# Seven small products for two large ones in an experts' first layer, other dispatch steps, and another filler

## The chip, the cores and the metric

The kernel runs on one core of one Trainium2 chip. The metric is the device time of one execution in microseconds (us), as the median of several runs. The engines are named as the profile names them: PE (TensorE, matrix products; PEld are its weight loads), DVE (VectorE), ACT (ScalarE), POOL (GpSimd) and SP (SyncE, which issues most transfers). PSUM is the memory that products are written to, in eight banks.

## The reference, cut to what matters

4096 tokens of width 512 pass through an attention over 3202 context rows and then through a mixture of eight experts, two for each token. Only the second half is touched by the change:

```python
def _L0_ffn_ref(x, w_router, b_router, w1, b1, w2, b2):
    ...
    cap = max(1, int(CAP_FACTOR * n / e))
    ...
    buf = jnp.zeros((e, cap, d), x.dtype).at[e_flat, posc].add(jnp.where(keep[:, None], xf[tok], 0.0))
    h = jax.nn.gelu(jnp.einsum('ecd,edf->ecf', buf, w1) + b1[:, None, :], approximate=False)
    out = jnp.einsum('ecf,efd->ecd', h, w2) + b2[:, None, :]
    og = out[e_flat, posc]
    w = jnp.where(keep, g_flat, 0.0).astype(x.dtype)
    y = jnp.zeros((n, d), x.dtype).at[tok].add(w[:, None] * og)
```

A token has a slot at each of its experts, `cap` is 640 slots, and the hidden width is 2048. All of it is computed in 32-bit floats.

## The kernel before, in words

There are three stages. The first is the attention, 1438 us, and the change doesn't touch it. The second ("routing") makes the attention's output for 32 tiles of 128 tokens, chooses experts and slots and writes the rows to the experts' slots in memory. The third runs the eight experts one after the other.

**Routing.** The tiles are taken in steps, `STEPS`, of 4, 4, 4, 4, 4, 3, 3, 2, 2, 2 tiles. A tile is 16 matmuls on PE (`tile_mm`, L1757), an add on DVE (`x1`) and a square sum on ACT. `scale` makes the step's `rstd` on POOL, `choose` picks the two experts on DVE and ACT and yields a mask, `place` counts with two matmuls (`pos`, L1872 and L1873) and gives each row its slot, and `dispatch` (POOL, an indirect transfer for each tile and choice, 64 in all) writes the rows. The order of these is written out by hand with `tc.issue_after`: a step is chosen while the next step's tiles are computed. `send(n)` issues n of the waiting dispatches. After the last tile, PE has no tiles left. There `idle_work` (L94) issues products of constants, 7 before the last `pos` and 1 behind it, and `first_expert_in` issues four products with a tile of zeros (L2152), the transposes of the first expert's five row tiles (`bps`, L85), more idle products, and the first expert's early products (`early_product`, L2118).

**An expert.** Its first layer is W1 (512 by 2048) times the 640 rows' transpose. It is done by the Strassen-Winograd scheme on blocks: `w1_forms` gives A11, A12, A22, S1, S2, A21 (in place S3), S4, and `XS` gives B11, B21, B22, T1, T2, T3, T4. With `HC` = 320 columns, `hidden(e, idx)` for idx 0 to 7 (`h`, `f` = half and quarter of the hidden width) makes seven products of two matmuls each, 128x128 by 128x320, on banks X, Q, Y, Z, W = 0, 1, 2 or 3, 4, 5. PE's order in an idx is X (0), Q (3), Y (4), X (1), Z (5), Y (6), W (2). The scheme's running sums are made by ACT, which copies a finished bank to the next one (Y<-X, L2210; p5<-Q, L2213; Z<-Y, L2216; W<-Z, L2223), where the next product is accumulated. DVE adds p5 to the two blocks that need it (L2224, L2226), and ACT applies the gelu, some of it in the next idx (`owed`). In expert 0, idx 0 to 3, the products X are done early, in the filler's time, and `early` holds them.

In between, DVE makes forms that are needed later: `w1_sums` (S1, S2, S3, S4 of the next idx's weights), and `left` and `right` (forms of the second layer). `dv`, `ac`, `ld` and `mm` each chain their instructions, so that every engine's order is that of the program. An in-order engine that waits for one instruction holds all behind it.

**The second layer** (`output`, `inner`, `deep`, `plain`, `rest`) uses two levels of the same scheme, with 128-column matmuls at its deeper level, whose forms DVE makes in 128x512 pieces. The next expert's rows are transposed inside it.

SP's queue loads the weights: `load_w1(e, h)` halves into two buffers in turn, `load_w2`, and `rows_in` for the next expert's rows.

Of the kernel before, what the change touches and what calls it, by code (L numbers as in the profile page):

```python
# [6 lines left out]
F32 = mybir.dt.float32  # L7
# [7 lines left out]
P = 128  # L15
# [5 lines left out]
def gated_layer(ctx, tc, x, x_t, ctxt, ctxt_t, ctxt_c, ctxt_r, g_xattn, g_ffn, w_sim, w_sim_r, b_sim, W_qv, W_qv_t, b_qv, b_qv_c, w_router, b_router, w1, b1, w2, b2, out):  # L21
# [37 lines left out]
    bsim = const.tile([P, 1], F32, name="bsim")  # L59
    gx = const.tile([P, 1], F32, name="gx")  # L60
    gf = const.tile([P, 1], F32, name="gf")
    zeros = const.tile([P, P], F32, name="zeros")
    nc.gpsimd.memset(zeros, 0.0)
    tgx, tgf = gx, gf

    qT_d = [dram.tile([P, DC, TG], F32, name=f"qT_d{g}", tag=f"qT_d{g}") for g in range(NG)]
# [1595 lines left out]
    with ExitStack() as s2:  # L1662
# [54 lines left out]
        scatters, middle, late = [], [], []  # L1717


        STEPS, sizes = [], [G] * (NT // G - 3) + [3, 3, 2, 2, 2]  # L1720
        for n in sizes:
            t = STEPS[-1][-1] + 1 if STEPS else 0
            STEPS.append(list(range(t, t + n)))
# [19 lines left out]
        def tile_mm(s, i):  # L1743
            t = s.tiles[i]
            g, q = divmod(t, 4)
            if g not in qTs:
                qTs[g] = sb.tile([P, DC, TG], F32, name=f"q2T{g}", tag="q2T")
                ld = nc.sync.dma_start(qTs[g], qT_d[g])
            r = sb.tile([P, 2, BW], F32, name=f"r2_{t}", tag="r2", bufs=6)
            ld = nc.sync.dma_start(r, r_d[t])  # L1750
            if t in (NT - 3 * G, NT - 1):
                with tc.issue_after(ld.ins):
                    load_w1(0, 0) if t < NT - 1 else load_w2(0, 0)
            ps = ps_mm.tile([P, 2, 512], F32, name=f"x1p{t}", tag="mm")
            for j in range(2):
                for c in range(DC):
                    mm = nc.tensor.matmul(  # L1757
                        ps[:, j, :B1], qTs[g][:, c, q * P : (q + 1) * P], W1[:, c, j, :], start=(c == 0), stop=(c == DC - 1)
                    )
            x1 = sb.tile([P, D], F32, name=f"x1_{t}", tag="x1", bufs=G + 2)  # L1760
            with tc.issue_after(chosen[-1]) if s.n == 2 and i else ExitStack():
                stt(
                    x1.rearrange("p (j d) -> p j d", j=2), ps[:, :, :256], tgx, r[:, :, :256], ALU.mult, ALU.add,
                    accum_out=s.sum[:, i : i + 1],
                )

            junk = sb.tile([P, D], F32, name=f"jx{t}", tag="jx", bufs=2)
            sq = nc.scalar.activation(
                junk, x1, AF.Square, scale=-float(D), bias=s.sum[:, i : i + 1], accum_out=s.ssd[:, i : i + 1]
            )  # L1770
            with tc.issue_after(sq.ins):
                nc.scalar.dma_start(out[t * P : (t + 1) * P, :], x1)

            l_ = s.lg[:, i, :]
            stt(
                l_.rearrange("p (j e) -> p j e", j=2), ps[:, 0, 256:B1].rearrange("p (j e) -> p j e", j=2), tgx,
                r[:, :, 256:], ALU.mult, ALU.add,
            )
            s.ldone = stt(l_, ps[:, 1, 256:B1], sd[:, t : t + 1], l_, ALU.mult, ALU.add)
            s.x1.append(x1)  # L1780
            return mm
# [7 lines left out]
        def choose(s):  # L1789
# [42 lines left out]


            s.g2 = T("gtwo", [P, n])
            nc.scalar.activation(s.g2, mx[:, 1, :], AF.Exp)
            s.gs = T("gs", [P, n])
            red(s.gs, gate, AX.X, ALU.add)
            for i, x1 in enumerate(s.x1):
# [83 lines left out]

        placed, chosen, w_ops = [], [], []

        idle = ps_id.tile([P, D], F32, name="idle", tag="idle")
        prev, s, scaled = None, begin(0), []
# [13 lines left out]
        for g in range(len(STEPS)):  # L1942
# [6 lines left out]
            if s.n > 2:  # L1949
                with tc.issue_after(mm.ins):  # L1950
                    place_prev()
                if s.n < G:
                    with tc.issue_after(scaled[-1].ins):
                        send(1)
                if s.n < G:

                    if not w_ops:
                        w_ops = w1_sums(0, 0)
                    with tc.issue_after(prev.placed.ins):
                        w_ops.pop(0)()  # L1960
                for i in range(ahead, s.n):
                    tile_mm(s, i)
            sc = scale(s)
            scaled.append(sc)
            if s.n == 2:
                with tc.issue_after(mm.ins):
# [12 lines left out]
                s.lift = small("lift", [P, s.n, E])  # L1979
                stt(s.lift[:, 0, :], cnt, 1.0 / P, second, ALU.mult, ALU.max)  # L1980
            with tc.issue_after(sc.ins):
                send(5 if s.next is None or s.next.n == 2 else 7 if s.n < G else 8)
            prev, s = s, s.next
        choose(prev)
        with tc.issue_after(idle_work(mm, 7).ins):
            place_prev()
        idle_work(prev.counted, 1)
        with tc.issue_after(prev.placed.ins):
            w_sum = w_ops.pop(0)()
        send(len(routed))  # L1990


# [5 lines left out]
    with ExitStack() as s3:  # L1998
# [112 lines left out]
        def early_product(second, f, B, cols, after, last=True):  # L2111

            A = [w1_forms(0, 0)[second][:, k, f * P : (f + 1) * P] for k in range(2)]
            pa = banks[2 + f][:, :HC]
            early[f] = sets[0][f].rearrange("p a b -> p (a b)")[:, :HC]
            for k in range(2):
                with tc.issue_after(after.ins):
                    after = nc.tensor.matmul(  # L2118
                        pa[:, cols], A[k], B[k][:, cols], start=False, stop=bool(second) and k == 1, skip_group_check=True
                    )  # L2120
            if not second:
                nc.scalar.copy(early[f][:, cols], pa[:, cols])
            elif last:
                tail["ac"] = nc.scalar.activation(hT[:, 0, f, :HC], pa, AF.Gelu, bias=b1_t[:, f : f + 1])
            return after
# [4 lines left out]
        def first_expert_in():  # L2130

            behind = None
            for s in range(NST):
# [13 lines left out]
                if behind is None:  # L2147

                    behind = prev.counted
                    for i in range(2, 6):  # L2150
                        with tc.issue_after(behind.ins):
                            behind = nc.tensor.matmul(  # L2152
                                banks[i], zeros, ident.unsqueeze(1).to_broadcast([P, 4, P]), start=True, stop=True
                            )
                        if i == 2:
                            with tc.issue_after(behind.ins):
                                ps = transposed(ps_tr, xb_of[0, s], f"bps0_{s}")
                            behind = moved[-1]
                else:
                    with tc.issue_after(behind.ins):  # L2160
                        ps = transposed(ps_tr, xb_of[0, s], f"bps0_{s}")
                dst = bT[:, :, s * P : (s + 1) * P]
                if s == NST // 2:
                    nc.scalar.copy(dst[:, :2, :], ps[:, :2, :])
# [1 line left out]
                        w_ops.pop(0)()  # L2166
                else:
                    (nc.vector.tensor_copy if s % 2 else nc.scalar.copy)(dst, ps)
                if s:
                    behind = idle_work(moved[-1], s, 2) if s <= NST // 2 else moved[-1]  # L2170
                cols = slice(0, P) if s == 0 else slice(P, HC)
                for q, f in {0: ORDER, NST // 2: ORDER[:5], NST - 1: ORDER[5:]}.get(s, ()):
                    B = [bT[:, k, :HC] for k in ((2, 3) if q else (0, 1))]
# [14 lines left out]

        stored, owed = [], []

        def hidden(e, idx):

            h, f = divmod(idx, KQ)
            col = e * NF + h * KH + f
            lo, hi = hT[:, 0, idx, :], hT[:, 1, idx, :]
            b_lo, b_hi = b1_t[:, col : col + 1], b1_t[:, col + KQ : col + KQ + 1]
            A = [[a[:, k, f * P : (f + 1) * P] for k in range(2)] for a in w1_forms(e, h)]
            X, Q, Y, Z, W = (banks[i][:, :HC] for i in (0, 1, 2 + idx % 2, 4, 5))
            p5 = p5s[idx % 2]
            there = e == 0 and f in early and h == 0  # L2200

            def product(ps, k, start=False):
                for i in range(2):
                    mm(ps, A[k][i], XS[{2: 6, 6: 2}.get(k, k)][i], start and i == 0, i == 1)

            if there:
                ac(lambda: nc.scalar.copy(Y, early.pop(f)))  # L2207
            else:
                product(X, 0, True)
                ac(lambda: nc.scalar.copy(Y, X))  # L2210
            product(Q, 3, True)
            ac(*owed[:1])
            ac(lambda: nc.scalar.copy(p5, Q))  # L2213
            ac(*owed[1:2])
            product(Y, 4)
            ac(lambda: nc.scalar.copy(Z, Y))  # L2216
            ac(*owed[2:])
            owed.clear()
            if not there:
                product(X, 1)  # L2220
                ac(lambda: nc.scalar.activation(lo[:, :HC], X, AF.Gelu, bias=b_lo))
            product(Z, 5)
            ac(lambda: nc.scalar.copy(W, Z))  # L2223
            dv(lambda: tt(hi[:, HC:], Z, p5, ALU.add))  # L2224
            product(Y, 6)
            dv(lambda: tt(lo[:, HC:], Y, p5, ALU.add))  # L2226
            product(W, 2)
            owed.extend([
                lambda: nc.scalar.activation(hi[:, HC:], hi[:, HC:], AF.Gelu, bias=b_hi),
                lambda: nc.scalar.activation(lo[:, HC:], lo[:, HC:], AF.Gelu, bias=b_lo),  # L2230
                lambda: nc.scalar.activation(hi[:, :HC], W, AF.Gelu, bias=b_hi),
            ])


        lo, hi = hT[:, 0], hT[:, 1]
# [86 lines left out]
        for e in range(E):  # L2322
# [23 lines left out]
            for idx in range(2 * KQ):  # L2346
                if more and idx == 2:
                    ld(*[lambda s=s: rows_in(e + 1, s) for s in range(NST - 1)])
                hidden(e, idx)
                if more and idx == KQ - 1:  # L2350
                    ld(lambda: load_w1(e + 1, 0))
                if 1 <= idx <= 4:
                    dv(*w1_sums(e, 1, idx - 1))
                if idx in (2, 4, 6):
                    dv(left(1, idx - 2, idx), left(3, idx - 2, idx))
                if idx == 3:
                    dv(right(1, 0, 4))
                if idx == 5:
# [172 lines left out]
```

## Time and profile before

| what | us | from |
|---|---|---|
| median of 3 runs (2563.48 to 2563.97) | 2563.72 | times |
| profiled execution, its own time | 2565.51 | times |
| profiled execution, span | 2563.7 | page |
| attention, to 1438.20 | 1438.2 | stretches |
| routing, 1438.20 to 1574.00; PE busy 129.62 | 135.8 | stretches |
| last `pos` to the first product of L2029, 1574.00 to 1591.45; PE busy 17.45 | 17.45 | stretches |
| experts, 1591.45 to 2558.00; PE busy 962.95 | 966.55 | stretches |
| one expert, 1707.61 to 1829.13 | 121.5 | timeline |

The granted clock of PE was 0.998 of full speed over the span. The page counts records: a matmul on 32-bit floats leaves two of them. A matmul's record lasts longer than the distance to the next one, since matmuls are pipelined; what a matmul costs in a stream is the distance from one start to the next. "x8" is a group of eight records; a bracket names the idle time before the group and what ended it.

### The profile page before, as it was taken

How to read it: one execution, taken by the hardware profiler on the slowest of the kernel's cores; microseconds unless marked ns; L12 is line 12 of the kernel's file. 1: busy time of each engine (PE TensorE's matmuls, PEld its weight loads, DVE VectorE, ACT ScalarE, POOL GpSimd, SP SyncE). 2: the span in 40 equal slices, each digit the busy share in tenths (PEclk: the TensorE clock that was granted, in tenths of full speed). 3: DMA queues.
4: the chain of work that ended last, by engine and by line, in shares of the span. 5: the costliest groups of instructions: out<-in, count | busy, mean ns of one | idle time of the engine just before them, and what ended most of it. 6: DMA issues, size and time to landing. Idle time of an engine off the chain costs nothing.

```text
span 2563.7 us, 36624 instructions
## 1 busy us (share of the span) xinstructions
PE 2543.1 (99%) x13964; PEld 2196.9 (86%) x13964; DVE 1844.5 (72%) x3670; ACT 693.2 (27%) x1459; POOL 275.9 (11%) x400
## 2 busy tenths in 40 slices
PE   9999999999999999999999999999999999999999
PEld 7788888998988989989989886787888878787978
DVE  8887965977877868759668666767675858484937
ACT  1112302223123123132230244323233232313140
POOL 0101220001001001000000066010101010101010
PEclk9999999999999999999999999999999999999999
DMA  7568795875976857759758795231314141414120
GB/s 260 197 214 299 270 346 168 288 255 177 315 232 207 284 192 263 258 180 304 244 166 281 274 350 202 83 128 66 132 67 156 46 160 38 161 42 156 50 99 21
DMA packets 198399, 488.99 MB, mean 191 GB/s; under 512 B 22462, under 2 KB 79102, under 8 KB 196176
## 3 DMA queue, kind: packets, MB, share of 16 engines
q1 hardware_dynamic: 151984, 386.37, 44.7%
q0 software_dynamic: 21696, 59.07, 6.4%
q10 hardware_dynamic: 24544, 41.21, 4.4%
q8 instruction: 110, 1.80, 0.3%
q14 instruction: 65, 0.53, 0.1%
HBM read 397.40 MB, written 97.52 MB: 193 GB/s over the span
## 4 chain that ended last, share of the span: by engine, by line
PE 88%; issue 5%; DVE 5%; POOL 1%; DMA 1%; ACT 0%; POOLq 0%; SPq 0%; another core or an unknown queue 0%; DVEq 0%; ACTq 0%
PE bank L2029 31%; PE bank L763 21%; PE bank L986 13%; PE bank L1155 6%; PE bank L1512 5%; PE x1p L1757 3%; PE bank L1256 2%; PE p7d L1512 1%; PE p4d L1512 1%; PE bank L815 1%; PE v L1256 1%; DVE SM L1025 1%; PE bank L992 1%; DVE hqT L1192 1%; PE bps L2105 1%
## 5 line engine op out<-in xcount | busy, mean ns | idle before, releaser
L763 PE MATMUL bank<-Qp,kt 128*128 128x256 f32 x1344 | 305.2, 379 | 0.0
L763 PEld LDWEIGHTS bank<-Qp,kt 128*128 128x128 f32 x1344 | 254.4, 190 | 34.1
L2029 PE MATMUL bank<-w,hT 128*128 128x256 f32 (+1 forms) x1280 | 260.7, 359 | 0.7 <-ACT u L2408 0.7
L2029 PEld LDWEIGHTS bank<-w,hT 128*128 128x128 f32 x1280 | 223.8, 190 | 27.4 <-ACT u L2408 1.1
L763 PE MATMUL bank<-q,kt 128*128 128x256 f32 x1008 | 231.3, 379 | 0.0
L2029 PE MATMUL bank<-bT,w 128*128 128x320 f32 x736 | 218.8, 433 | 2.0 <-ACT bank L2216 1.6
L763 PEld LDWEIGHTS bank<-q,kt 128*128 128x128 f32 x1008 | 191.5, 190 | 26.0
L2224 DVE TENSOR_TENSOR hT<-bank,l 128x320 f32<-128x320 f32 x64 | 31.5, 492 | 253.4 <-ACT bank L2223 253.4
L986 PE MATMUL bank<-dt,vf 128*128 128x128 f32 x1680 | 204.8, 275 | 0.0
L986 PEld LDWEIGHTS bank<-dt,vf 128*128 128x128 f32 x1680 | 196.0, 192 | 0.0
L2029 PEld LDWEIGHTS bank<-bT,w 128*128 128x128 f32 x736 | 139.0, 190 | 60.6 <-ACT bank L2216 3.1
L2029 PE MATMUL bank<-XT,w1s 128*128 128x320 f32 x512 | 148.4, 433 | 0.0
L806 DVE TENSOR_TENSOR M<-M,E_all 128x1024 f32<-128x1024 f32 x80 | 97.8, 1223 | 47.8 <-ACT E_all L723 46.4
L2029 PEld LDWEIGHTS bank<-XT,w1s 128*128 128x128 f32 x512 | 97.2, 190 | 40.6 <-ACT bank L2207 0.4
L2397 POOL DMA_INDIRECT out<-acc,ti x40 | 39.6, 990 | 819.2 <-DVE acc L2342 812.5
L1757 PE MATMUL x1p<-W,q2T 128*128 128x264 f32 x512 | 119.8, 396 | 0.5 <-DVE p1d L1527 0.5
L1757 PEld LDWEIGHTS x1p<-W,q2T 128*128 128x128 f32 x512 | 98.8, 195 | 18.0 <-DVE p1d L1527 0.9
L719 DVE TENSOR_TENSOR E_all<-bank,p5s 128x512 f32<-128x512 f32 x42 | 28.9, 689 | 114.5 <-ACT bank L718 114.5
L893 DVE TENSOR_TENSOR E_all<-E_all,mb 128x1024 f32<-128x1024 f32 x84 | 101.2, 1211 | 10.3 <-ACT mb L868 10.3
L986 PE MATMUL bank<-E_all,vf 128*128 128x128 f32 x828 | 106.5, 275 | 0.0
L894 ACT ACTIVATE E_all<-E_all 128x1024 f32<-128x1024 f32 x84 | 88.8, 1057 | 49.8 <-DVE E_all L893 49.3
L986 PEld LDWEIGHTS bank<-E_all,vf 128*128 128x128 f32 x828 | 99.8, 192 | 0.3
(602 smaller groups left out, 4755.9 us busy)
## 6 DMA issues: line engine op xcount, KB each, us to landing
vf<-vf_d SPq DMA_DIRECT2D x122, 768.0 KB
kt<-kt_d SPq DMA_DIRECT2D x84, 512.0 KB
w<-in_w SPq DMA_DIRECT2D x16, 2048.0 KB
w<-in_w SPq DMA_DIRECT2D x32, 1024.0 KB
kt<-in_ctxt_t SPq DMA_DIRECT2D x84, 384.0 KB
wp<-wt_d SPq DMA_DIRECT2D x56, 520.0 KB
buf_d<-zero SPq DMA_DIRECT2D x80, 129.0 KB
xb<-buf_d SPq DMA_DIRECT2D x39, 258.0 KB
```

The lines of the kernel that those rows point to most:

```text
L763: nc.tensor.matmul(ps[:, jl, :], kts[j][:, KSLOT[p], k, :], B[p][:, k, :], start=start and jl == 0 and k == 0, stop=stop and k == 1, skip_ ...
L806: tt(M, M, e[:, :, h], ALU.max)
L893: live[g]["last"] = tt(e, e, m, ALU.subtract)
L894: live[g]["exp"] = nc.scalar.activation(e, e, AF.Exp)
L986: nc.tensor.matmul(ps, a[:, j, :], rhs[r][:, j, :], start=start and j == 0, stop=j == NP - 1 and (rest is None or add is None), skip_group ...
L1155: nc.tensor.matmul(ps[b], vt[:, j - i * JH, b * P : (b + 1) * P], right(j) if j < NJ else right_c, start=start and j == 0 and b == 0, stop ...
L1256: mm = nc.tensor.matmul(acc[k][:, b, :], a[:, b * P : (b + 1) * P], r, start=start and b == 0, stop=stop, skip_group_check=True,)
L1512: nc.tensor.matmul(ps[m], A[p][:, k, m * P : (m + 1) * P], wt[:, k, :], start=start and k == 0, stop=stop and k == DC - 1, skip_group_chec ...
L1757: mm = nc.tensor.matmul(ps[:, j, :B1], qTs[g][:, c, q * P : (q + 1) * P], W1[:, c, j, :], start=(c == 0), stop=(c == DC - 1))
L2029: return chained("pe", lambda: nc.tensor.matmul(ps, a, b, start=start, stop=stop, skip_group_check=True))
L2224: dv(lambda: tt(hi[:, HC:], Z, p5, ALU.add))
L2397: sc = nc.gpsimd.indirect_dma_start(out=out[:, :], out_offset=rows_of(ti, s), in_=accs[s][:, :], in_offset=None, bounds_check=N - 1, oob_i ...
```

## The change

It has three parts.

1. *Split.* In the first layer, idx 0 to 5, products 6 (S4 by B22) and 2 (A22 by T4) are no longer made by two matmuls of 320 columns each. For every two neighbouring idx (a pair, 0 to 2), each of these two products is one block product of 256 rows (of the hidden width), 256 (of the model width) and 320 columns, and is computed by seven products of 128x128 by 128x160 with the scheme once more (`parts`). `deep_w` and `deep_x` make its forms on DVE, four adds each, in buffers of the second layer's sets. A part runs in idx 1 (product 6 of pair 0), 2 (product 2 of pair 0), 3, 4, 5, 6; in each, its pieces `first`, `second`, `third` stand between the idx's other products. The three regions X', W', Q' of a part share one bank of the transposes' pool, and Y', Z' share bank 5 (bank 3 at idx 6). Two copies on ACT carry the running sums (Y'<-X', Z'<-Y'), and four adds on DVE put the part onto the rows of hT; its gelus come an idx later. In expert 0's idx 1 to 3, PE's order becomes X', Q', W', Y (4), Y', X', Q (3), Z', Y', Z (5).
2. *Steps.* 4, 4, 4, 4, 3, 3, 3, 3, 2, 2 instead of 4, 4, 4, 4, 4, 3, 3, 2, 2, 2, with other numbers of dispatches sent at each step; the first two tiles' `x1` of every step of fewer than four wait for the choice of the step before. The sums of the first expert's weights move from the steps to the tail.
3. *Filler.* `idle_work` issues 11 instead of 7 products of constants, then 4 instead of 1; the four products with zeros, and the tile `zeros`, go; two more follow the first transposes. A gelu on one column is put behind the last choice's exponential.

Beside these, `load_w1(e + 1, 0)` moves from idx 3 to idx 4, and the `left` forms from idx 2, 4, 6 to idx 4, 6, 7.

```diff
-        STEPS, sizes = [], [G] * (NT // G - 3) + [3, 3, 2, 2, 2]
+        STEPS, sizes = [], [G] * (NT // G - 4) + [3, 3, 3, 3, 2, 2]
...
-            with tc.issue_after(chosen[-1]) if s.n == 2 and i else ExitStack():
+            with tc.issue_after(chosen[-1]) if s.n < G and i < 2 else ExitStack():
...
-                send(5 if s.next is None or s.next.n == 2 else 7 if s.n < G else 8)
+                send(len(routed) if s.next is None else 4 if s.n == 2 else 7)
             prev, s = s, s.next
         choose(prev)
-        with tc.issue_after(idle_work(mm, 7).ins):
+        with tc.issue_after(prev.last_exp.ins):
+            nc.scalar.activation(small("gelu", [P, 1]), ones[:, 0:1], AF.Gelu)
+        with tc.issue_after(idle_work(mm, 11).ins):
             place_prev()
-        idle_work(prev.counted, 1)
-        with tc.issue_after(prev.placed.ins):
-            w_sum = w_ops.pop(0)()
+        idle_work(prev.counted, 4)
+        w_ops = w1_sums(0, 0)
...
-                    for i in range(2, 6):
-                        with tc.issue_after(behind.ins):
-                            behind = nc.tensor.matmul(
-                                banks[i], zeros, ident.unsqueeze(1).to_broadcast([P, 4, P]), start=True, stop=True
-                            )
...
-                if s:
-                    behind = idle_work(moved[-1], s, 2) if s <= NST // 2 else moved[-1]
+                behind = idle_work(moved[-1], s or 2, 2 if s else 4) if s <= NST // 2 else moved[-1]
...
+        DEEP_IDX = 6
+        HH = HC // 2
...
+        def deep_x(k):
+            b, (t1, t2, t4, t3) = x_of[k]
+            b11, b12, b21, b22 = (b[:, c, d : d + HH] for c in range(2) for d in (0, HH))
+            return [
+                lambda: tt(t1, b12, b11, ALU.subtract),
+                lambda: tt(t2, b22, t1, ALU.subtract),
+                lambda: tt(t3, b22, b12, ALU.subtract),
+                lambda: tt(t4, b21, t2, ALU.subtract),
+            ]
+        def deep_w(e, k, pair):
...
+            return [
+                lambda: tt(s1, a21, a22, ALU.add),
+                lambda: tt(s2, s1, a11, ALU.subtract),
+                lambda: tt(a21, a11, a21, ALU.subtract),
+                lambda: tt(s4, a12, s2, ALU.subtract),
+            ]
+        def parts(e, k, pair, c_bank):
+            XWQ = ps_tr.tile([P, DC, P], F32, name=f"d{e}_{k}{pair}", tag="tr").rearrange("p c t -> p (c t)")
+            X, W, Q = (XWQ[:, i * HH : (i + 1) * HH] for i in range(3))
+            YZ = banks[c_bank][:, : 2 * HH]
+            Y, Z = YZ[:, :HH], YZ[:, HH:]
...
+            def first():
+                mm(X, a11, b11, True, True)
+                ac(lambda: nc.scalar.copy(Y, X))
+                mm(Q, s1, t1, False, True)
+                mm(W, a22, t4, False, True)
+            def second():
+                mm(Y, s2, t2, False, True)
+                ac(lambda: nc.scalar.copy(Z, Y))
+                mm(X, a12, b21, False, True)
+            def third():
+                mm(Z, s3, t3, False, True)
+                mm(Y, s4, b22, False, True)
...
+            split = idx < DEEP_IDX
+            if 1 <= idx <= DEEP_IDX:
+                k, pair = ("6", idx // 2) if idx % 2 else ("2", idx // 2 - 1)
+                part = parts(e, k, pair, 5 if split else 2 + (idx + 1) % 2)
...
+            if not split:
+                product(Y, 6)
+                dv(lambda: tt(lo[:, HC:], Y, p5, ALU.add))
+                product(W, 2)
...
-                if more and idx == KQ - 1:
+                if more and idx == KQ:
                     ld(lambda: load_w1(e + 1, 0))
                 if 1 <= idx <= 4:
                     dv(*w1_sums(e, 1, idx - 1))
-                if idx in (2, 4, 6):
-                    dv(left(1, idx - 2, idx), left(3, idx - 2, idx))
+                if idx == 0:
+                    dv(*deep_w(e, "6", 0), *deep_x("6"), *deep_w(e, "2", 0), *deep_x("2"))
+                if idx == 1:
+                    dv(*deep_w(e, "6", 1), *deep_w(e, "2", 1))
+                if idx == 4:
+                    dv(*deep_w(e, "6", 2), *deep_w(e, "2", 2))
+                if idx in (4, 6, 7):
+                    k = (0, 2, 4)[(4, 6, 7).index(idx)]
+                    dv(left(1, k, k + 2), left(3, k, k + 2))
```

## The prediction

> **What bounds the kernel now.** I read the busy totals, then the chain of waits, then the groups that belong to the diff.
>
> ```profile
> PE 2543.1 (99%) x13964; PEld 2196.9 (86%) x13964; DVE 1844.5 (72%) x3670; ACT 693.2 (27%) x1459; POOL 275.9 (11%) x400
> ...
> PE 88%; issue 5%; DVE 5%; POOL 1%; DMA 1%; ACT 0%; POOLq 0%; SPq 0%; another core or an unknown queue 0%; DVEq 0%; ACTq 0%
> ...
> L2029 PE MATMUL bank<-bT,w 128*128 128x320 f32 x736 | 218.8, 433 | 2.0 <-ACT bank L2216 1.6
> L2224 DVE TENSOR_TENSOR hT<-bank,l 128x320 f32<-128x320 f32 x64 | 31.5, 492 | 253.4 <-ACT bank L2223 253.4
> ```
>
> TensorE sets the time: a matmul removed is worth its own issue time, and a wait put in front of a matmul costs its full length. The two halves of one expert differ on VectorE (columns: stretch, length, then busy time of PE, PEld, DVE, ACT, POOL):
>
> ```profile
> 1707.61:1768.00 60.39, 60.39 (x227) 42.66 (x226) 26.68 (x56) 28.16 (x63) 6.95 (x7) 1.00 0.43 157
> 1768.00:1829.13 61.13, 61.13 (x430) 57.68 (x428) 56.34 (x112) 8.23 (x26) 3.06 (x4) 1.00 0.15 53
> ```
>
> The first layer (`hidden`, first row) leaves VectorE idle for 33.7 us, the second layer almost nothing. So extra VectorE work in `hidden` is affordable as a sum, and only its order can hurt. The timeline of one block gives the durations (columns: start, duration):
>
> ```profile
> 1716.23 2.32 PE L2029 MATMUL bank<-XT,w1s 128*128 128x320 f32 x8
> 1716.43 0.41 ACT L2210 COPY bank<-bank 128x320 f32<-128x320 f32 x1 [2.82 <-PE bank L2029]
> ...
> 1718.38 2.32 PE L2029 MATMUL bank<-bT,w 128*128 128x320 f32 x8
> ...
> 1720.54 1.24 PE L2029 MATMUL bank<-bT,w1s 128*128 128x320 f32 x4
> 1720.79 0.41 ACT L2223 COPY bank<-bank 128x320 f32<-128x320 f32 x1 [0.60 <-PE bank L2029]
> 1721.23 0.49 DVE L2224 TENSOR_TENSOR hT<-bank,l 128x320 f32<-128x320 f32 x1 [6.47 <-ACT bank L2223]
> ```
>
> Eight records take 1718.38 - 1716.23 = 2.15 us, 269 ns each; a program matmul is two. ScalarE's copy begins 0.25 us after the product has ended (1720.79 against 1720.54). VectorE's add on the same bank begins 0.03 us after that copy's end: accesses to one bank are put in a row. And at one place ScalarE's copy isn't covered, in expert 0:
>
> ```profile
> 1591.45 2.45 PE L2029 MATMUL bank<-XT,w1s 128*128 128x320 f32 x8
> ...
> 1593.99 0.41 ACT L2216 COPY bank<-bank 128x320 f32<-128x320 f32 x1 [0.84 <-PE bank L2029]
> ...
> 1594.46 1.34 PE L2029 MATMUL bank<-bT,w 128*128 128x320 f32 x4 [0.55 <-ACT bank L2216]
> ...
> 1595.64 1.24 PE L2029 MATMUL bank<-bT,w1s 128*128 128x320 f32 x4
> ```
>
> PE's last record lasts 433 ns but the next could issue after 269, so PE was free at 1593.90 - 0.16 = 1593.74, restarted at 1594.46 (0.72 later), and the four records after the gap took 1.18 instead of 1.08 us. A product that waits for the copy of the one just before it loses 0.72 + 0.10 = 0.82 us.
>
> **The split: gain.** In idx 0 to 5 products 6 and 2 (8 records of 320 columns per idx) go; idx 1 to 6 each get seven matmuls of 160 columns (14 records). 160 columns have no row. The 128-column row runs at 111.7 ns (eight records in 0.89 us), the 256-column row at 216, the 320-column row at 269: one line within 1%, so 137.5 ns. Its far bounds, 111.7 and 216, would be -0.59 and +0.87 us a split; I take the line, with 5 ns either way. Per split 8 x 0.269 - 14 x 0.1375 = 0.227 us; 48 splits give -10.9 us, 1.37 an expert. The 128-column matmuls reach 111.7 while their weight loads last 190, so 14 loads are no bound.
>
> **The split: the new wait.** `parts.first` issues X', then the copy Y'<-X', then Q' and W', and X', W', Q' lie in one bank. By the order of instructions the changed kernel's Q' waits for exactly that copy, in all six splits; behind Q' on PE stand all later products. It is the uncovered copy of expert 0, with 160 columns: between the 128-column copy (0.25) and the 320-column one (0.41) lies 0.28, so 0.82 - 0.13 = 0.69 us. Bounds: 0.42 (the profile's idle of 0.55 less 0.13) and 0.82. Idx 2, 3, 4, 6 have this alone: 4 x 0.69 = 2.76.
>
> The Trainium skill ("PSUM — Partial Sum Buffer", section "PSUM bank collisions raise a hardware error") says that two engines may not touch one bank in the same partitions together, other columns included. The 0.03 us above agrees for VectorE and ScalarE; by a rule of addresses alone Q' would need no wait, and the sum would be 32 x 0.69 = 22 us smaller (at idx 1 and 5 the forms below hold PE anyway).
>
> **The split: late forms.** At idx 1 the forms are late. They are queued on VectorE behind the high-half add of idx 0, which starts 0.69 us after that idx's Z product (1721.23 - 1720.54). SBUF adds: 128x256 last 0.42, start 0.34 apart, 0.45 if dependent; 128x512 last 0.69; on that line 128 columns start 0.21 apart (0.31 dependent), 160 columns 0.24 (0.35). After the hi add (0.40) come four of 128 (0.94) and t1, t2, t3, t4 (0.35 + 0.24 + 0.24 + 0.32): W' can start 3.2 us after Z, and was wanted after X, X', Q', at 1.08 + 0.55 = 1.63. The stall, Q's included, is 1.6, with the restart 1.7 us (bounds: 0.69, and 2.8, where product X doesn't lie ahead of it).
> At idx 5 `deep_w` for the third pair stands behind the hi add of idx 4 and the four `w1_sums` of 128x256 (1.47): s1 is ready at 0.69 + 0.40 + 1.47 + 0.28 = 2.84, Q' wanted at 1.36: 1.55 with the semaphore, 1.65 us with the restart (bounds 0.69 and 2.1).
>
> The Trainium skill ("Vector Engine (DVE) Microarchitecture Reference", section 5.2) prices a stream of such adds at 1.04 ns a column plus 75 ns; the eight of idx 1 would take 1.8 instead of 2.1 us and the sum would fall by some 2 us. [...]
>
> **The split: hidden parts.** Four VectorE adds (1.7 us) and two small copies per split lie in idle time: 26.7 + 17 of some 65 us. `left` forms move to idx 4, 6, 7 and make the second layer's first forms 1.4 us later; in this profile they end at 1777.9 and are used at 1783.5, so 5.6 us cover them. If that were gone, 1.4 us an expert, 11 us. Loading the next w1 moves on SP from idx 3 to 4, ahead only of loads for later; its transfer takes some 6 us and is first read by `w1_sums` 15 us on: nothing.
>
> **Expert 0** has no product X in idx 1 to 3: idx 1 costs 1.08 more (2.8), but Q now lies between copy and Z there, which removes three of the old 0.8 us stalls.
>
> Experts: seven times 2.76 + 1.7 + 1.65 - 1.37 = 4.74, 33.2; expert 0: 2.8 + 2.76 + 1.65 - 2.4 - 1.37 = 3.4. Together +36.6 us.
>
> **Steps and tail.**
>
> ```profile
> 1557.55 0.36 PE L1872 MATMUL pos<-mask,upper 128*128 128x16 f32 x2 [2.60 <-DVE mask L1845]
> ...
> 1567.90 6.25 PE L94 MATMUL idle<-ident,ones 128*128 128x512 f32 x14
> ```
>
> PE loses 0.68 + 0.21 + 1.48 + 1.09 + 2.60 = 6.1 us waiting for routing. With 3,3,3,3,2,2 the masks of steps of three are chosen beside three tiles of 3.58 us each; laid out by hand with the trace's times (mask 3.2 us after rstd, place 2.1, a dispatch 1.28) two stalls stay, 1.7 and 1.5, and more hidden gaps close: `first` ends at 1560.4 instead of 1567.87. The tail behind it is gapless on PE, 23.58 us to the first product, and gets filler: idle products 7 to 11, 1 to 4, two more, less the four of `zeros`, net +5 of 0.868 (14 records in 6.08) = +4.3. So -7.4 + 4.3 = -3.1 us. The new mask would be there at 1567.9, the 11 idle ones end at 1570.0: they, not VectorE, would set it. Bounds: -6 and +3. Dispatch on POOL (the last ended 1582.92) and the Gelu table load (1.28) stay inside the tail.
>
> The sum is +33.5 us: 2565.51 (the profiled execution, span 2563.7) becomes 2599.0; against the median, 1.8 lower, 2597.
>
> **Rivals.**
> 1. *Only half the wait* (9%): ScalarE's copy is mostly covered and the forms come in time at idx 5. 32 waits at 0.35 us and 16 at 0.9 (idx 1 and 5): 11.2 + 14.4 - 10.9 - 2.4 - 3.1 = +9.2: 2573. For it: 1600.61 shows PE's idle as 0.50, less than 0.72. Against: PE's restart stands 0.06 us behind the copy's end.
> 2. *Faster* (7%): VectorE and ScalarE are ahead and the split costs no wait: -10.9 - 2.4 - 3.1: 2547. For it: ScalarE is idle 73%. Against: the copy can't start before X' has ended, whatever its load. It becomes likely if Q' doesn't wait.
> 3. *The second layer starves* (9%): its 92% busy VectorE takes the late forms badly, 1.4 us an expert: 2608; from 5.6 us of lateness on it decides.
> 4. *The steps cost* (3%): a late tile and the filler both lie on the path, +3 instead of -3: 2603.
>
> Forecast: 72%, itself 2584 to 2610. The range 2575 to 2609 cuts off rival 2, half of rival 1 and the far end of rival 3. A measurement here can tell 0.2%, 5.1 us. Faster 0.07, same 0.04 (rival 1 with smaller waits), slower 0.89.
>
> **What would show it.** In the changed profile PE should have idle of 0.4 to 0.7 us before the `d` tile's second matmul in every split, put down to ScalarE's copy, larger in idx 1 and 5 and put down to VectorE's forms; an expert's period of 126 us instead of 121.5; 160-column records 137 ns apart; the first product of L2029 near 1588. A period under 121.5 would make me wrong.

## The result, and the profile after

The changed kernel takes 2612.57 us (median of 5 runs, 2609.41 to 2613.68) against 2563.48 before (2561.88 to 2563.97): a ratio of 1.0188, 95% interval 1.0176 to 1.0200. It is 49 us slower. The direction was forecast; the time lies 3.6 us above the range, which ended at 2609. The profiled executions differ by 45.0 us in their spans (2608.7 against 2563.7).

The page of the changed kernel, busy totals and chain:

```profile
PE 2549.3 (98%) x14262; PEld 2218.0 (85%) x14262; DVE 1977.0 (76%) x4118; ACT 712.1 (27%) x1556; POOL 275.4 (11%) x399
...
PE 85%; issue 6%; DVE 6%; DMA 2%; POOL 1%; ACT 1%; POOLq 0%; SPq 0%; another core or an unknown queue 0%; DVEq 0%; ACTq 0%
```

PE has 298 records more, and only 6 us more busy time, on a span that is 45 us longer. So the time went into PE standing still. The chain agrees: PE's share falls from 88% to 85%, and those of DVE, DMA, ACT and "issue" rise by a point each. Who held PE in the tail and the experts, from 1570 on, without two rows under 1 us (columns: who waited, on whom, us in all, how often, the longest):

```profile
PE d L2027 <- ACT bank L2231: 13.6, 29, 1.1
PE d L2027 <- DVE l L2209: 11.6, 8, 1.5
PE d L2027 <- ACT hT L2328: 6.6, 7, 1.0
PE bps L2103 <- DMA xb<-buf_d: 6.1, 7, 1.0
PE d L2027 <- DVE l L2196: 2.0, 1, 2.0
PE d L2027 <- DVE l L2199: 1.6, 7, 0.2
PE d L2027 <- issue: 1.3, 3, 0.4
```

`d` is the bank of X', W', Q'. Line 2231 is the copy Y'<-X', 2209 the form s1, 2196 and 2199 the forms t1 and t4. The first and the last row together are the copy's waits: 32, in idx 2, 3, 4 and 6 of eight experts. The second row is idx 5, the fifth and the sixth are idx 1. Line 2328 is a gelu that stands on ACT behind the copy, and its row is idx 1 of experts 1 to 7:

```profile
1721.33 0.28 ACT L2231 COPY bank<-d 128x160 f32<-128x160 f32 x1
1721.51 0.58 ACT L2328 ACTIVATE hT<-hT,b_t 128x320 f32<-128x320 f32 x1
...
1721.73 0.32 DVE L2196 TENSOR_TENSOR l<-bT 128x160 f32<-128x160 f32 x1
...
1722.19 0.51 PE L2027 MATMUL d<-l,l 128*128 128x160 f32 x2 [0.95 <-ACT hT L2328]
```

When Q' starts here, the copy has been done for 0.58 us. The gelu ended at 1722.09 and t1 at 1722.05. Q' does not need the gelu: in the block shown next it starts while that gelu runs. So t1 held it, and these 6.6 us belong to the late forms. The run with two banks, below, confirms it: without any copy's wait, the same 6.6 us in seven waits stand at line 2196.

The fourth row is new and was not in the forecast: the transposes of the next expert's last row tile wait for their rows. In the profile before this wait cost 0.9 us once in the whole kernel.

One block of expert 1 with nothing but the copy's wait (timeline; start, duration):

```profile
1737.75 0.43 PE L2027 MATMUL d<-bT,w1s 128*128 128x160 f32 x2
1737.95 0.41 ACT L2300 COPY bank<-bank 128x320 f32<-128x320 f32 x1 [0.65 <-PE bank L2027]
...
1738.27 0.28 ACT L2231 COPY bank<-d 128x160 f32<-128x160 f32 x1
1738.46 0.57 ACT L2328 ACTIVATE hT<-hT,b_t 128x320 f32<-128x320 f32 x1
...
1738.61 0.54 PE L2027 MATMUL d<-l,l 128*128 128x160 f32 x2 [0.42 <-ACT bank L2231]
...
1738.99 0.43 PE L2027 MATMUL d<-l,w1s 128*128 128x160 f32 x2
...
1739.26 1.24 PE L2027 MATMUL bank<-XT,w1s 128*128 128x320 f32 x4
```

X' starts at 1737.75; two records of 160 columns take 0.27 us (1738.99 to 1739.26), so Q' was due at 1738.02. It starts at 1738.61, 0.06 behind the end of the copy, and takes 0.11 longer than its 0.27: 0.69 us, the price in the forecast. Note what the profile's bracket says: 0.42. It counts from the modelled end of the last record, not from when the next could have issued, and leaves out the slow restart.

The sums of such excesses, start to start of PE's records beyond their usual distance, in the two profiled executions (the first row is the price of the records instead, 0.1375 us each in the forecast and 0.136 measured):

| term | forecast, us | measured, us |
|---|---|---|
| fewer columns: measured, 48 x (8 x 0.269 - 14 x 0.136) | -10.9 | -11.9 |
| stalls of the splits, experts 1 to 7 | +42.8 | +43.0 |
| stalls of the splits, expert 0 | +7.2 | +9.8 |
| expert 0's old stalls, removed | -2.4 | -2.3 |
| last row tile late (7.2, less 1.0 before) | 0 | +6.2 |
| routing and tail, up to the first product of L2029/L2027 | -3.1 | -0.25 |
| sum (the spans: +45.0) | +33.6 | +44.6 |

### The profile page after: what moved, and what is told of

The parts are those of the page before. It is cut to its first block, busy times and chain, and to the rows that moved or that the text cites. A ratio compares the mean times of both kernels' runs of the same rounds, so it can differ in the third digit from the quotient of the medians.

```text
span 2608.7 us, 37874 instructions
## 1 busy us (share of the span) xinstructions
PE 2549.3 (98%) x14262; PEld 2218.0 (85%) x14262; DVE 1977.0 (76%) x4118; ACT 712.1 (27%) x1556; POOL 275.4 (11%) x399
## 4 chain that ended last, share of the span: by engine, by line
PE 85%; issue 6%; DVE 6%; DMA 2%; POOL 1%; ACT 1%; POOLq 0%; SPq 0%; another core or an unknown queue 0%; DVEq 0%; ACTq 0%
PE bank L2027 28%; PE bank L761 20%; PE bank L984 12%; PE bank L1153 6%; PE bank L1510 5%; PE bank L1254 2%; PE x1p L1755 2%; PE d L2027 2%; PE p7d L1510 1%; PE p4d L1510 1%; PE bank L813 1%; PE v L1254 1%; DMA xb<-buf_d 1%; PE bps L2103 1%; DVE SM L1023 1%
## 5 line engine op out<-in xcount | busy, mean ns | idle before, releaser
L2027 PE MATMUL bank<-w,hT 128*128 128x256 f32 (+1 forms) x1280 | 260.7, 359 | 0.7 <-ACT u L2519 0.7
L2027 PEld LDWEIGHTS bank<-w,hT 128*128 128x128 f32 x1280 | 223.8, 190 | 27.4 <-ACT u L2519 1.1
L2027 PE MATMUL bank<-bT,w 128*128 128x320 f32 x736 | 211.1, 432 | 0.6 <-ACT bank L2309 0.6
L2027 PEld LDWEIGHTS bank<-bT,w 128*128 128x128 f32 x736 | 136.6, 190 | 50.5 <-ACT bank L2309 1.1
L2027 PE MATMUL bank<-XT,w1s 128*128 128x320 f32 x512 | 157.3, 435 | 0.0
L2027 PEld LDWEIGHTS bank<-XT,w1s 128*128 128x128 f32 x512 | 92.5, 191 | 25.6 <-issue 0.4
L891 DVE TENSOR_TENSOR E_all<-E_all,mb 128x1024 f32<-128x1024 f32 x84 | 101.4, 1214 | 10.3 <-ACT mb L866 10.3
L2317 DVE TENSOR_TENSOR hT<-bank,l 128x320 f32<-128x320 f32 x48 | 23.6, 492 | 101.0 <-ACT bank L2309 92.8
```

The source lines that it names most:

```text
L891: live[g]["last"] = tt(e, e, m, ALU.subtract)
L2027: return chained("pe", lambda: nc.tensor.matmul(ps, a, b, start=start, stop=stop, skip_group_check=True))
```

## The experiments

Every run beside the kernel before on the same chip, which took 2557.8 to 2566.9 us there; what counts is the difference.

**The split taken out.**

```diff
-        DEEP_IDX = 6
+        DEEP_IDX = 0
...
-                if idx == 0:
-                    dv(*deep_w(e, "6", 0), *deep_x("6"), *deep_w(e, "2", 0), *deep_x("2"))
...
-                if idx in (4, 6, 7):
+                if idx in (2, 4, 6):
```

> Routing steps, filler and the order of expert 0's first four blocks as in the changed kernel; no split, and the forms of the second layer where they were before. My theory: the split carries the whole loss. Routing and tail gain nothing (first product at 1591.2 against 1591.45 us), expert 0 loses three old stalls of 0.76 us, so 2561 us, between 2558 and 2564. Rival: steps and filler cost several us themselves, 2568 or more.

Measured: 2565.31 against 2565.44, ratio 0.9999 (0.9989 to 1.0008): no difference that can be told. The loss is the split's, with the moves of `left` and `load_w1` that this run takes back too. The expected 2561 us were missed. The gain of 2.5 us was there in the experts' stretch (963.6 against 966.6 us in the profiles) and was lost in front of it: the first product of the experts started at 1594.5 instead of 1591.45. So the new steps and filler cost some 3 us in this run, where the forecast had them gain 3; 1.4 us of it is idle time at the early products (at 1583.24) that the changed kernel's profile doesn't have.

**The copy behind Q' and W'.**

```diff
                 mm(X, a11, b11, True, True)
-                ac(lambda: nc.scalar.copy(Y, X))
                 mm(Q, s1, t1, False, True)
                 mm(W, a22, t4, False, True)
+                ac(lambda: nc.scalar.copy(Y, X))
```

> The changed kernel with the copy Y'<-X' issued behind the part's products Q' and W' instead of ahead of them, nothing else. My theory: Q' waits for that copy only because it follows it in the same bank; the wait of 0.69 us goes in idx 2, 3, 4, 6 of every expert (32 x 0.69 = 22 us, and 1 to 2 us more in expert 0), and idx 1 and 5 keep theirs, which late forms hold. 2612.6 - 23.5 = 2589 us, 2584 to 2594. Rival: the copy's latency only moves to the next product in that bank (Y'), or small products are slow in themselves: 2604 or more.

Measured: 2590.02 us (before: 2565.44), where 2589 was expected. All of PE's waits in its experts, from 1600 on:

```profile
PE d L2027 <- DVE l L2209: 10.8, 8, 1.4
PE d L2027 <- DVE l L2196: 7.9, 8, 1.9
PE bps L2103 <- DMA xb<-buf_d: 5.3, 7, 0.8
PE d L2027 <- DVE l L2199: 2.3, 8, 0.3
PE bank L2027 <- ACT u L2519: 0.7, 1, 0.7
```

No wait of a part for ACT is left: the next product in need of the copy is Y', which has Q (1.08 us) ahead of it. The forms' waits stand, as expected; at idx 1 the profile now puts all eight down to t1 (line 2196).

**The forms earlier.** The first sixteen ahead of block 0's adds, the last eight at idx 3.

```diff
+                if idx == 0:
+                    dv(*deep_w(e, "6", 0), *deep_x("6"), *deep_w(e, "2", 0), *deep_x("2"))
                 hidden(e, idx)
...
-                if idx == 0:
-                    dv(*deep_w(e, "6", 0), *deep_x("6"), *deep_w(e, "2", 0), *deep_x("2"))
...
-                if idx == 4:
+                if idx == 3:
                     dv(*deep_w(e, "6", 2), *deep_w(e, "2", 2))
```

> The changed kernel with the first sixteen small forms on VectorE ahead of block 0's high add instead of behind it, and the last eight at block 3 instead of 4; copies as they were. My theory: in idx 1 and 5 the stall falls from 1.67 to the copy's 0.69 us, 7 x 2 x 0.98 = 13.7 us, expert 0's idx 1 some 1.5 us: 2612.6 - 15 = 2597.5 us, 2593 to 2602. Rival: VectorE's queue gets no shorter and the forms are late elsewhere (no less than 2608).

Measured: 2597.80 us, where 2597.5 was expected. From 1600 on no wait for DVE is left, and the copy's is now at all six places (the 42 of the first row and six of the third; two rows of 0.7 us, once each, are left out):

```profile
PE d L2027 <- ACT bank L2231: 19.3, 42, 1.0
PE bps L2103 <- DMA xb<-buf_d: 5.9, 7, 0.9
PE d L2027 <- issue: 2.8, 7, 0.4
```

**The row load earlier.**

```diff
-            dv(right(4, 0, 8))
             if more:
                 dv(*coefs(e + 1, (0,)))
+            dv(right(4, 0, 8))
+            if more:
                 ld(lambda: rows_in(e + 1, NST - 1))
```

> The changed kernel with the four small operations that free the row buffer, and the row load behind them, ahead of the last large right-hand form (2.28 us on VectorE) instead of behind it. My theory: the transposes of the next expert's last rows wait 7 x 1.04 = 7.2 us for that load because VectorE is late in the second layer; the load goes out 2.3 us sooner and the wait goes: 2612.6 - 7 = 2605.5 us, 2603 to 2608. Rival: the load waits for something else than VectorE (no change, 2612), or the large form is then late for its product (2613 or more).

Measured: 2605.66 us, where 2605.5 was expected, and the wait of `bps` is gone. So the load had waited for DVE; whether the small forms or the move of `left` made DVE late, no run separates. The place, in the changed kernel (timeline):

```profile
1809.73 2.28 DVE L2366 TENSOR_TENSOR w<-w,XT 128x2048 f32<-128x2048 f32 x1
1811.93 0.15 DVE L2091 CAST ti<-xb 128x1 int32<-128x1 f32 x1
...
1812.55 0.34 SPq L2038 DMA_DIRECT2D xb<-buf_d  x1
...
1815.49 0.63 PE L2103 MATMUL bps<-ident,xb 128*128 128x128 f32 x4 [0.98 <-DMA xb<-buf_d]
```

and the same place before:

```profile
1799.48 0.14 DVE L2093 CAST ti<-xb 128x1 int32<-128x1 f32 x1
...
1800.09 0.34 SPq L2040 DMA_DIRECT2D xb<-buf_d  x1
...
1802.95 0.60 PE L2105 MATMUL bps<-ident,xb 128*128 128x128 f32 x4
```

Four small DVE operations read the row tile whose buffer the load needs. Before, SP issued the load 2.86 us ahead of the transposes, and the transposes found the rows; after, they found them 2.94 us behind its issue, having waited 0.98 us. The load takes nearly all of these 2.9 us: the old kernel had next to no slack at this place, while its forms, queued on the same engine, had 5.6 us.

These three expectations were made from 2612.6 us. As differences to the kernel before, the three kernels stand at +24.6, +32.4 and +40.2 us, and the changed kernel at +45.0 on the same chip (below): 20.4, 12.6 and 4.8 us less, where 23.5, 15 and 7 were expected. So the closeness of the totals is partly luck. The prices are not: the experts' stretch in the profiles, from their first product to PE's last, is 1011.8 us in both profiles of the changed kernel, and 988.2, 995.4 and 1005.2 us here, which is 23.5, 16.4 and 6.6 less. What is missing lies ahead of the experts, which begin at 1594.4, 1595.5 and 1594.7 us in these profiles and at 1591.2 and 1591.8 in the changed kernel's.

**The three together, and with other routing.** The first has the changed kernel's routing and the three edits above; the second has the routing, filler and order of the tail from before; the third is the first with a shorter filler:

```diff
-        with tc.issue_after(idle_work(mm, 11).ins):
+        with tc.issue_after(idle_work(mm, 8).ins):
             place_prev()
-        idle_work(prev.counted, 4)
+        idle_work(prev.counted, 1)
```

> The changed kernel with the later copy, the earlier forms and the earlier row load together. My theory: nothing of the split's price is left but its instructions, so its gain shows: 48 x 0.248 us = 11.9 us against the kernel with the new steps and filler but no split (2565.3 us beside a before of 2565.4): 2553.5 us, and up to 4 us more for expert 0, whose forms VectorE can't make earlier: 2551 to 2558. Rival: the three share a cover, and the wait returns elsewhere (VectorE's forms of the second layer, 1 us an expert or more): 2561 or more, no faster than before.

> The kernel before, its steps and filler untouched, with the split and the three corrections, and the changed order in expert 0's first blocks. My theory: steps and filler give nothing or cost up to 3 us, so this is as fast as the one with the new routing or up to 3 us faster: 2565.4 - 11.9 - 2.3 = 2551 us, 2548 to 2556. Rival (the prediction's own step): the new routing gains 3 us, and this one is 3 us slower than that.

> As the first of these three, with 8 instead of 11 products of constants ahead of the last count and 1 instead of 4 behind it (6 x 0.868 = 5.2 us of PE). My theory: the last choice is ready 2 to 2.6 us before the 11 products end, so part of the filler lies on the path: 2 to 5 us faster than with the long filler, 2549 to 2552. Rival: the filler only covers a wait for the rows that stands anyway (no change).

| kernel | median, us | ratio to before (2557.84) | interval | experts in the profile, us | their first product at |
|---|---|---|---|---|---|
| three edits | 2547.54 | 0.9960 | 0.9946 to 0.9973 | 954.25 | 1586.04 |
| and the old routing | 2546.59 | 0.9953 | 0.9940 to 0.9967 | 954.25 | 1583.85 |
| and the short filler | 2544.37 | 0.9950 | 0.9936 to 0.9964 | 954.26 | 1582.61 |

The kernel before was itself 6 to 9 us faster on this chip than beside the other runs, so the absolute expectations (made from 2565.4) lie too high; the differences to it are -10.3, -11.3 and -13.5 us where -12 (-14 to -7), -14 (-17 to -9) and, for the third, 2 to 5 us below the first were expected. The experts' stretch is 12.3 us shorter than before: 11.9 for the split, 2.3 for expert 0's old stalls and 1.0 for the old wait for rows, less some 3 that expert 0's idx 1 to 3 still lose. Of PE's waits from 1600 on one of 0.7 us is left. The three edits turn a kernel 1.8% slower than before into one 0.4% faster, and the third kernel of the table, 0.5% faster than before, beats both kernels of this case.

As to routing: on this one chip, new steps with the long filler reach the experts 2.2 us later than the old routing in the profiles; 6 idle products fewer (5.2 us) bring 3.2 us in the medians.

**The changed kernel again, the split alone, and two banks.** The second is the kernel before with only the split (and expert 0's order). The third gives X' a bank of its own, the copy staying ahead of Q'; beside the lines shown, Q' now begins its bank anew, and one add on DVE becomes two:

```diff
-            XWQ = ps_tr.tile([P, DC, P], F32, name=f"d{e}_{k}{pair}", tag="tr").rearrange("p c t -> p (c t)")
-            X, W, Q = (XWQ[:, i * HH : (i + 1) * HH] for i in range(3))
+            XA, WQ = (
+                ps_tr.tile([P, DC, P], F32, name=f"d{n}{e}_{k}{pair}", tag="tr").rearrange("p c t -> p (c t)") for n in "xw"
+            )
+            X, (W, Q) = XA[:, :HH], (WQ[:, i * HH : (i + 1) * HH] for i in range(2))
```

> The changed kernel itself, on the same chip as the next two. My theory: 45 to 49 us over the kernel before (ratio 1.018), the last 4 us being the spread of routing and tail from one execution to the next. Rival: the 4 us between the profile's difference (45) and the medians' (49) belong to the change, and it stands at 49 again.

> The kernel before with the split as the change has it (and expert 0's changed order), its own steps and filler. My theory: the split with its waits is the whole loss, 45.2 us in the experts' stretch of the profile: 45 us over before, within 3 us of the changed kernel. Rival (the prediction's sum): steps and filler hide 3 us and the split alone costs 37; or they cost several us themselves, and this is 5 or more below the changed kernel.

> The changed kernel with X' in a bank of its own and Q' and W' in another, the copy Y'<-X' where it was, ahead of Q'; one add on VectorE becomes two. My theory: the wait belongs to the shared bank and not to the place of the copy in the order, so it goes as with the later copy: 23 us below the changed kernel, 18 to 25 (the split add costs VectorE 0.2 us a part, and X' and Q' now wait for the part before to be added). Rival: ScalarE's place in the order makes the wait, and it stays (within 4 us of the changed kernel).

Beside a before of 2566.94 us they took 2611.92 (ratio 1.0176, 1.0159 to 1.0193), 2610.53 (1.0173, 1.0156 to 1.0190) and 2590.10 us (1.0094, 1.0078 to 1.0111). The changed kernel stands at +45.0 us here, so 4 us of the result's +49 are not a constant of the change; where they come from was not followed. (In the result's pair, the profiled execution of the kernel before was 2.0 us above its median, and that of the changed kernel 2.1 below.) The split alone makes +43.6 of it; the 1.4 us left for steps and filler can't be told from nothing in these runs. With two banks the kernel is 21.8 us faster than the changed one, about as with the later copy. PE's waits from 1600 on in that kernel:

```profile
PE dw L2027 <- DVE l L2209: 11.6, 8, 1.5
PE dw L2027 <- DVE l L2196: 6.6, 7, 0.9
PE bps L2103 <- DMA xb<-buf_d: 5.8, 7, 0.9
PE dw L2027 <- DVE l L2199: 1.9, 8, 0.3
PE bank L2027 <- ACT u L2522: 0.7, 1, 0.7
PE dx L2027 <- DVE hT L2248: 0.4, 2, 0.2
```

No wait of a part for ACT is left, though the copy is issued where it was. (The 0.7 us in the second layer stand in the kernel before as well; the last row is X' waiting for the part before to be added.) So the wait came with the shared bank and not with the copy's place. The Trainium skill has this as a rule in "PSUM — Partial Sum Buffer", section "PSUM bank collisions raise a hardware error": a program is to guard accesses to PSUM by bank (more exactly, by bank and group of partitions) and not by address. The trace agrees: in the changed kernel Q' touches other columns than the copy reads, and waits all the same, 0.69 us. A tile of this pool is one bank, so no run here tells a wait by bank from a wait by tile.

## Why the prediction was right, and where it failed

*The gain of the split* was 11.9 instead of 10.9 us: 160 columns run at 136 ns a record, the line through the other widths gave 137.5. Right.

*The copy's wait* was 0.69 us in every clean block, as forecast, and two independent edits remove it. The other signs held too, nearly: records of 160 columns 136 ns apart (137 forecast), an expert's period of 127.3 us (126), the late rows making the difference, and the experts' first product at 1591.2 (1588).

*The late forms* cost 1.67 (idx 1) and 1.68 us (idx 5) in expert 1, forecast 1.7 and 1.65. The eight adds of idx 1 took 2.08 us on DVE (1720.80 to 1722.88). The row price in the forecast was 2.1; the Trainium skill's stream price ("Vector Engine (DVE) Microarchitecture Reference", section 5.2) had given 1.8, and here the measurement decides for the row: the adds of this list start 0.31 us (128 columns) and 0.35 us (160) apart where one reads the result of the one before, and 0.21 to 0.24 elsewhere.

*The hidden parts* is the step that failed. It put forms 1.4 us late in the second layer at nothing, since 5.6 us cover them, and rival 3 was to decide only from that much lateness on. The lateness was rightly seen, and its price was looked for at the first forms' product alone. Behind the forms, on the same in-order queue, stand four operations of 0.15 to 0.22 us that free a row buffer; behind these a load on SP; behind the load a transpose on PE. That chain had next to no slack, and 0.9 to 1.1 us an expert came out there: +6.2 us, the largest error of the sum. The run with the earlier row load takes it away. Without it the time would have been about 2606 us, inside the range. It is not the only error: expert 0 (+2.6) and steps and tail (+2.9) cost more than forecast, the columns saved 1.0 more, and the medians differ by 4 us more than the two profiles. With the +45.0 us that the changed kernel showed later, the time would have been 2608.5, just inside the range, so that chance had a part in where it fell.

*Expert 0* was 2.6 us dearer than forecast. Its idx 1 lost 4.1 us instead of 2.8: Q' came 2.2 us late, and most of the 1.9 us behind it is a slower clock, told below. Its idx 2 and 3 lost 1.4 and 1.25 instead of 0.69, since there ACT starts the small copy later (1.2 and 1.1 us after X' instead of 0.5), behind a copy of 320 columns.

*Steps and tail* were mis-sized: -3.1 forecast, -0.25 in the profiles, +3 in the run without the split. The tail's extra filler was right (27.6 us from the end of `first` to the first product in the changed kernel's profile, 27.9 forecast). The gain ahead of it was not: `first` ended 4.5 us earlier, not 7.5. PE's idle time around the counts fell from 6.1 only to 4.9 us, where two stalls of 3.2 us together were to stay (this is the changed kernel's PE):

```profile
1508.85 0.41 PE L1870 MATMUL pos<-mask,upper 128*128 128x32 f32 x2 [0.96 <-DVE rv L1828]
...
1510.86 10.92 PE L1755 MATMUL x1p<-W,q2T 128*128 128x264 f32 x48 [0.99 <-DVE lg L1773]
...
1553.27 0.37 PE L1870 MATMUL pos<-mask,upper 128*128 128x24 f32 x2 [1.31 <-issue]
```

Of the 4.5 us, 3.4 are two stretches at half the clock in the old routing's profile (last section), which the changed kernel's routing doesn't have. Nor are the stalls of the old routing, on which the gain was reckoned, the same from run to run: PE stood idle for 3.0 us at the counts in the run with the three edits and the old routing, and for 7.1 in the run of the split alone. What delays the masks in some runs was not followed.

*The rivals.* Half the wait and a faster kernel are refuted by the clean blocks. The starving second layer was true as a mechanism, at another place and at 0.9 us an expert net. Steps that cost, the rival with the smallest chance, came nearer than the forecast's gain: the experts begin at 1591.2 to 1595.5 us in the seven profiles with new steps and long filler beside a before of 2563 to 2567 us, and at 1591.0 and 1591.45 in the two with the old ones.

## What to carry to other kernels

Before splitting products into smaller ones, look at what stands between each product and its copy: here, two products that follow each other in one bank with another engine's copy between cost 0.69 us each time, and either another order or another bank was the cure. Ask of a named wait whether what it names had to be waited for: the gelu of line 2328 had not. When a queue gets later, follow every consumer behind it, loads issued on its behalf included, and take the slack of the tightest. A gain of 0.25 us a split is smaller than any uncovered wait of this kernel, so the order has to be worked out before the arithmetic pays.

## What the runs showed of the hardware

After a stall PE ran at half its clock for a few microseconds. In the changed kernel's expert 0, Q' of idx 1 came 2.2 us late at 1597.85, and in the stretch behind it the granted clock was 0.55 (columns: stretch, length, busy times, then the clock):

```profile
1597.80:1601.60 3.80, 3.75 (x10) 2.72 (x11) 2.67 (x11) 0.03 (x1) 2.30 (x3) 0.55 0.99 347
1601.60:1605.00 3.40, 3.40 (x18) 2.57 (x16) 1.24 (x3) 1.19 (x4) 0.00 (x0) 1.00 0.71 269
```

The kernel before has it too, in the routing, behind idle times of 1.48 and 2.60 us:

```profile
1538.50:1541.90 3.40, 3.40 (x10) 2.56 (x10) 2.40 (x9) 0.21 (x2) 2.79 (x3) 0.54 1.00 344
...
1558.90:1562.20 3.30, 3.30 (x9) 2.56 (x8) 2.00 (x11) 0.81 (x2) 0.74 (x2) 0.52 0.23 86
```

Each costs 1.7 us or so on top of the stall (records of 264 columns 440 ns apart instead of 223, eight of them). The mean clock of the whole span, 0.998, hides it. The idle times of 1.45 us in idx 5 of all eight experts never set it off.

The traces' records of the granted clock show more. Such a stretch lasts 3.41 us (once twice that), and in each of the six profiles with more than one of them ahead of the kernel's end, they begin whole multiples of 3.41 us apart (6, 13, 14 or 27). The Trainium skill ("TensorE: Matmul & The Clock Gate", section "What's actually happening") gives about 3.4 us as the idle window after which the clock halves; here an idle time of 1.48 us was enough once and 1.45 us not at eight other places, so the length of one stall doesn't decide alone. Where on that grid it falls may; no run here isolated it.
